# Moving cache gathers, patches and key turns in a four-layer residual kernel

## The chip, the core and the metric

The kernel runs on one core of a Trainium2 chip. The metric is device time in microseconds (us) of one launch. The kernel is written engine by engine: TensorE does matrix products and transposes, VectorE and ScalarE elementwise work and the copies out of PSUM, GpSimd some elementwise work and all gathers and scatters (indirect DMAs), and SyncE (SP) starts most of the plain DMAs; ScalarE starts some too.

## The reference

The input x has 64 sequences of 64 tokens of 512 numbers. Four layers are added to it one after the other, all in float32:

```python
x = x + einsum('bct,bcd->bdt', x, w0[cond])                 # one 64x64 mixer per sequence
x = x + x @ W_base.T + lora(x)                              # low-rank path picked per sequence
q, k, v = heads(x)                                          # 8 query heads, 4 key/value heads of 64
q, k = rope(rms(q)), rope(rms(k))
k_blocks = k_blocks.at[blk, :, off, :].set(k)               # new tokens written into a paged cache
v_blocks = v_blocks.at[blk, :, off, :].set(v)
x = x + softmax(mask(q @ k_all.T * SCALE)) @ v_all @ Wo.T   # window of 256 positions
x = x + x @ W3.T + low_rank3(x)
```

The cache is read through a table of 257 blocks of 16 positions per sequence. Sequences can share blocks, so a token written for one can be read by another. The mask leaves 256 positions, so for a sequence at most 21 blocks matter.

## The kernel before

The whole order of the work is written out by hand, and each engine runs its instructions in that order. An instruction that waits holds back everything behind it on its engine.

**First phase.** 39 rounds (line 882, n from 0 to 38) over tiles of 128 tokens, of which there are 32 (NTILE). Rounds 0 to 31 do the mixers and the first low-rank layer in groups of four, then keys and values (`product_kv`, line 815). The new rows of tile n - 1 are normalised and turned in the next round (`new_rows`, line 823) and scattered into two DRAM tables, pv and pk (`put_rows`, line 831), which hold a copy of every cache block that is written in this call. Those scatters are on GpSimd. Queries are done eleven rounds later: `product_q` (258), `norm_q` (266), whose last multiply (line 248) is on GpSimd for most tiles, and `turn_q` (276), which transposes them and writes them to DRAM (qd). Rounds 28 to 31 do no queries; rounds 32 to 38 do only queries.

**Cache reading.** For groups of four sequences, `k_load` (148) gathers old key blocks into kt, 84 rows of 8 KB per call, two calls per group. `k_copy` (154) reorders them into k2, a quarter at a time; the quarter with o4 = 3, and all of the first two groups, on ScalarE, others on VectorE. `k_patch` (161) gathers from pk over the rows of k2 that were written in this call. `k_turn` (169) transposes a quarter of one head pair into the one PSUM bank psK, and copies it into kT_mem, on ScalarE if o4 is even and on VectorE if it is odd. For one sequence, `v_load` (186) issues four gathers of values into vs_mem, which has two slots; `v_copy` (195) copies them on ScalarE into vt_mem, which has four slots; `v_patch` (199) gathers from pv over them; `v_share` (204) has SP issue three small DMAs within vt_mem.

**Second phase.** 128 steps (line 1117): a step is a sequence b and one of two pairs of key heads (gp), eight steps make a group q of four sequences, and i is the step within the group. In each step TensorE computes the scores of the next step (`scores`, 975), turns the shares of this one (`turn_p`, 1019), turns keys of the next group (`turn1`, then `turn2` further down, by the table in line 1114), does a part of the last layers of the group before (line 1144, `last_parts`), in the first two groups also the remaining queries, and at last multiplies shares by values (`values`, 1035). ScalarE and VectorE go along: `maxima` (990), `exponentials` (1004), `shares` (1011), `keep_p` (1028, the copy pT), `window` (967, the mask), `keep_o` (1045).

Of the kernel before, what the change touches and what calls it, by code (L numbers as in the profile page):

```python
# [21 lines left out]
NTILE = NT // P  # L22
# [28 lines left out]
def kernel(  # L51
# [89 lines left out]
    def bank(pool, name):  # L141
        return pool.tile([P, 512], F32, name=name, tag="b")
# [5 lines left out]
    def k_load(q, h):  # L148

        if q < B // 4:  # L150
            gather(kt[:NP, 2 * h : 2 * h + 2].rearrange("p g o d -> p (g o d)"), k_halves,
                   ik_old[:, h, q : q + 1])

    def k_copy(q, o4):

        if q < B // 4:
            (S.copy if o4 == 3 or q < 2 else V.tensor_copy)(
                k2[:NP].rearrange("p (oq o) g d -> p oq o g d", o=4)[:, :, o4],
                kt[:NP].rearrange("p g (oq o) d -> p oq o g d", o=4)[:, :, o4])

    def k_patch(q):

        if q < B // 4:
            gather(k2[:NP].rearrange("p o g d -> p (o g d)"), pk, ik_new[:, q : q + 1], NWR - 1)

    def kT(q, gp):
        return kT_mem[q % 2][:, gp].rearrange("p (b o c i) -> p b o c i", b=4, o=3, c=4)

    def k_turn(q, gp, o4, pool=psK):

        if q >= B // 4:
            return
        ps = bank(pool, f"psk{q}_{gp}_{o4}")[:, : 4 * NP].rearrange("p (o r) -> p o r", o=4)
        for oq in range(4):
            PE.transpose(ps[:, oq, :],  # L175
                         k2[:NP, 4 * oq + o4, 2 * gp : 2 * gp + 2].rearrange("p g d -> p (g d)"),
                         ident[:NP, :NP])
        if o4 < 3:
            dst = kT(q, gp)[:, :, o4, :3]
        else:  # L180
            dst = kT(q, gp)[:, :, :, 3]
        copy = V.tensor_copy if o4 % 2 else S.copy
        copy(dst[:, :, :, :NR], ps[:, :3].rearrange("p c (b j) -> p b c j", b=4))
        copy(dst[:, :, :, NR:], ps[:, 3].rearrange("p (b c j) -> p b c j", b=4, c=3))  # L184

    def v_load(b):
        if b < B:
            for g in range(NG):
                gather(vs_mem[:NV, b % 2, g].rearrange("p o d -> p (o d)"), v_rows,
                       iv_old[:, b, g : g + 1])  # L190
# [4 lines left out]
    def v_copy(b):  # L195
        if b < B:
            S.copy(vt(b)[:NV], vs_mem[:NV, b % 2].rearrange("p g o d -> p o g d"))  # L197

    def v_patch(b):
        if b < B:  # L200
            gather(vt_mem[:NV, b % 4], pv.rearrange("w (q r) -> (w q) r", q=4),
                   iv_new[:, b : b + 1], NWR * 4 - 1)

    def v_share(b):

        if b < B:
            for c in range(3):
                DMA.dma_start(out=vt(b)[96:NVK, c], in_=vt(b)[32 * c : 32 * c + 28, 3])
# [5 lines left out]
    def queries(n):  # L214

        return n - LQ if n < NTILE - 4 else -1 if n < NTILE else n - 4 - LQ
# [49 lines left out]
    def norm_q(n):  # L266

        if not 0 <= n < NTILE:
            return lambda: None
        rest = turned(n, psq.pop(n), NH, qsc, "q", qp1, qp2)  # L270

        def second():
            qheads[n] = rest()
        return second
# [19 lines left out]
    with ExitStack() as one:  # L294
# [587 lines left out]
        for n in range(NLAST):  # L882
            if n % 4 == 0:
                parts = first_parts(n // 4 + 1)
            w_load0(n + 12)
            x2_load(queries(n + 2))
            if 1 <= n <= NTILE:
                new_rows(n - 1)
            if n != NTILE:
                norm_q(queries(n - 1))()  # L890
            lag = 4 if n < 20 else 3 if n < 22 else 2 if n < 24 else 1
            while done["p"] <= min(n - lag, NTILE - 1):
                put_rows(done["p"])
                done["p"] += 1
            if n == NTILE:
                k_patch(0)
                v_patch(0)
                v_patch(1)
                norm_q(queries(n - 1))()
            product_q(queries(n), psP)  # L900
            if n % 4:
                x_load0(n + 8)
            if n in (14, 16, 18, 20):
                gather_indices((n - 14) // 2)
            if n < NTILE:
                parts[n % 4]()
            if n % 4 == 0:
                x_load0(n + 8)
            if n == 1:
                written_rows()  # L910
                places()
            if n in (1, 2):
                for o4 in (0, 1):
                    fill_copy(2 * (n - 1) + o4)
            if n == 2:
                fill_store(pv)
            if n >= 2:
                winners(n + 1 + max(0, (n - 6) // 4))
            if 2 <= n < 8:
                zero_rows((pk, pv)[n % 2], n // 2 - 1)  # L920
            if n in (13, 15, 17, 19):
                index_lists((n - 13) // 2)
            if n % 4 == 3:
                mixers(n // 4 + 2)
            if 5 <= n < 10:
                late_inputs(n - 5)
            if 14 <= n < 18:
                positions(n - 14)
            if n == 19:
                adapters(ad3_i, sc3b, 8, mask3)  # L930
                middles()
            if n == 21:
                residual3()
                G.memset(sm_mem, 0.0)
            turn_q(queries(n - 5 if n == NTILE else n - 2 if n != NTILE - 3 else -1), psO)
            if n < NTILE:
                product_kv(n)
            if n in (NTILE - 13, NTILE - 12):
                k_load(0, n - (NTILE - 13))
            if n in (NTILE - 11, NTILE - 9):  # L940
                v_load((n - (NTILE - 11)) // 2)
            if n in (NTILE - 7, NTILE - 5):
                v_copy((n - (NTILE - 7)) // 2)
            if NTILE - 8 <= n < NTILE - 4:
                k_copy(0, n - (NTILE - 8))
            if n in (NTILE - 3, NTILE - 2):
                k_load(1, n - (NTILE - 3))
            if n == NTILE - 4:
                v_load(2)


    def pool2(name, bufs):
# [5 lines left out]
    def q_load(q):  # L958
        if q < B // 4:
            qts[q] = ap2.tile([P, 2, 4, 2, T], F32, name=f"qs{q}", tag="qs")  # L960
            DMA.dma_start(out=qts[q], in_=qd[:, q])
# [73 lines left out]
    def values(s):  # L1035

        q, b, gp = steps[s]
        po = bank(psO, f"po{s}")[:, :P]
        for o in range(3):
            for g in range(2):  # L1040
                PE.matmul(po[g * HD : (g + 1) * HD, :], lhsT=vt(b)[:NVK, o, 2 * gp + g],  # L1041
                          rhs=pTs[s][g][:, o, :], start=(o == 0), stop=(o == 2))
        return po

    def keep_o(s, po):
        q, b, gp = steps[s]
        if s % 8 == 0:
            oTs[q] = ap2.tile([P, 2, 4, 2, T], F32, name=f"oT{q}", tag="oT")
        S.copy(oTs[q][:, gp, b % 4].rearrange("p h t -> p (h t)"), po)
# [59 lines left out]
    shares(0)  # L1109
    norm_q(nq - 1)()  # L1110
    window(1)
    for o4 in range(3):
        k_copy(1, o4)
    turns = {3: (None, (0, 0)), 4: ((1, 0), (0, 1)), 5: ((1, 1), (0, 2)), 6: ((1, 2), (0, 3)),
             7: ((1, 3), None)}
# [1 line left out]
    for s, (q, b, gp) in enumerate(steps):  # L1117
        i = s % 8
        turn1, turn2 = turns.get(i, (None, None))
        if i == 0 and q:  # L1120
            x_load(q)
        if i == 2:
            q_load(q + 1)
        if gp == 0:
            v_load(b + 3)
        else:
            v_share(b + 1)
            v_patch(b + 2)
        if i == 1:
            k_patch(q + 1)  # L1130
        if i in (2, 3):
            k_load(q + 2, i - 2)
        scores(s + 1)
        turn_p(s)
        if 0 < s < 16:
            turn_q(nq + s - 2, psO)
        if turn1:
            k_turn(q + 1, *turn1)
        maxima(s + 1)
        keep_p(s)  # L1140
        exponentials(s + 1)
        second = norm_q(nq + s if q < 2 else -1)
        if parts:
            parts.pop(0)()
        if q < 2:
            product_q(nq + s + 1, psM)
            x2_load(nq + s + 3)
        shares(s + 1)
        second()
        if gp:  # L1150
            window(b + 2)
        po = values(s)
        if turn2:
            k_turn(q + 1, *turn2)
        keep_o(s, po)
        if gp == 0:
            v_copy(b + 2)
        if i == 0:
            k_copy(q + 1, 3)
        elif i > 4:  # L1160
            k_copy(q + 2, i - 5)
        if i == 7:
            parts += last_parts(q)
    for part in parts:
# [52 lines left out]
```

## Time and profile before

| | |
|---|---|
| median of three runs | 1236.24 us (1232.07 to 1236.6) |
| the profiled execution | 1225.52 us, span 1223.7 us |
| TensorE busy | 1107.0 us, 90% of the span |
| VectorE, ScalarE, GpSimd busy | 753.0, 571.2, 613.9 us |
| value gathers (256, line 65) | 310.2 us of GpSimd, 1212 ns each |
| mean granted clock of TensorE | 0.976 |

The profiled execution is one run; its time is what its own lines add up to, and the median of the separate runs is 0.9% above it. Times within the profile are counted from the start of the span. In the slices each digit is the busy share of 30.6 us in tenths. A line of the timeline gives start, duration, engine, line of the kernel, operation, what is written and read, the number of instructions merged, and in brackets how long the engine sat idle before it and what ended that. The ends of TensorE's products are modelled, so its busy time is an upper bound. Gathers and scatters all carry line 65 or 71, since a helper issues them; they are told apart by their tiles: vs_mem for v_load, kt for k_load, k from pk for k_patch, vt_mem from pv for v_patch, pv and pk from va and k for the scatters.

### The profile page before, as it was taken

The page shows a single profiled execution, that of the slowest core. Times are in us where ns is not written, and L with a number is a line of the kernel's source. Part 1 is how long each engine was busy: PE and PEld are TensorE (multiplying, and loading weights), DVE is VectorE, ACT ScalarE, POOL GpSimd, SP SyncE. Part 2 cuts the span into 40 slices and gives each one's busy share as a digit, 9 for nine tenths or more (in the row PEclk, how much of TensorE's full clock was granted, in tenths as well). Part 3 has the DMA queues.
Part 4 walks back from the last instruction along what each step waited for, and adds up shares of the span by engine and source line. Part 5 has one row for each costly group of instructions (what it writes and reads, how often), then busy time and mean ns, then how long its engine had stood idle before and what let it go on. Part 6 is the DMA issues. An engine that isn't in the chain of part 4 may idle for free.

```text
span 1223.7 us, 17686 instructions
## 1 busy us (share of the span) xinstructions
PE 1107.0 (90%) x5622; PEld 639.8 (52%) x5622; DVE 753.0 (62%) x2313; ACT 571.2 (47%) x1472; POOL 613.9 (50%) x601
## 2 busy tenths in 40 slices
PE   4998899999999968879989989999999899999998
PEld 4434444444444434446656656555655565665665
DVE  3775346766666755875665655665665665666561
ACT  1332222232233324555655655655665565666651
POOL 3243323332543351887566666656656656656620
PEclk9999899999899988998999999999999999999999
DMA  8375713234331363546546556556555745756420
GB/s 270 123 258 209 241 41 113 74 102 131 111 114 51 108 171 111 157 117 147 129 113 161 130 126 143 147 126 142 147 127 140 167 121 121 161 139 150 99 64 35
DMA packets 129820, 163.20 MB, mean 133 GB/s; under 512 B 58079, under 2 KB 96891, under 8 KB 125545
## 3 DMA queue, kind: packets, MB, share of 16 engines
q0 software_dynamic: 63872, 85.04, 28.5%
q1 hardware_dynamic: 46416, 53.89, 14.5%
q10 hardware_dynamic: 19440, 23.15, 5.6%
q8 instruction: 45, 0.74, 0.3%
q14 instruction: 47, 0.39, 0.1%
HBM read 139.66 MB, written 50.33 MB: 155 GB/s over the span
## 4 chain that ended last, share of the span: by engine, by line
PE 66%; DVE 8%; issue 7%; DMA 6%; POOL 6%; ACT 3%; ACTq 0%; POOLq 0%; DVEq 0%; SPq 0%
PE pso L1059 9%; PE pp L1025 8%; PE po L1041 7%; PE psc L983 7%; PE ps L787 5%; PE psy L1084 5%; PE q L263 5%; PE kv L820 5%; PE psk L175 4%; PE psy L1078 4%; PE psxa L1067 2%; PE psy L1086 2%; DMA pv<-vt_mem,zidx 2%; POOL vs_mem L65 2%; PE ps L789 2%
## 5 line engine op out<-in xcount | busy, mean ns | idle before, releaser
L65 POOL DMA_INDIRECT vs_mem<-in_vblk_dram,iv_old x256 | 310.2, 1212 | 77.4 <-issue 70.5
L1009 ACT ACTIVATE sm_mem<-sm_mem,mn 128x336 f32<-128x336 f32 x256 | 145.6, 574 | 32.5 <-DVE mn L999 26.9
L65 POOL DMA_INDIRECT vt_mem<-pv,iv_new x64 | 80.0, 1250 | 160.2 <-ACT vt_mem L197 84.0
L999 DVE CUSTOM_DVE_ANT_0 sm_mem<-psc,pen 128x336 f32<-128x336 f32 x256 | 119.6, 501 | 43.6 <-PE pp L1025 22.8
L1041 PEld LDWEIGHTS po<-pT,vt_mem 124*64 124x64 f32 x1536 | 84.9, 137 | 87.0 <-ACT sm_mem L1009 49.2
L1041 PE MATMUL po<-pT,vt_mem 124*64 124x128 f32 x1536 | 118.4, 282 | 12.5 <-ACT pT L1032 7.3
L1059 PE MATMUL pso<-oT,woT_sb 128*128 128x256 f32 x512 | 123.2, 385 | 0.0
L263 PE MATMUL q<-wq_sb,x2q 128*128 128x512 f32 x256 | 120.8, 617 | 1.9 <-DMA x2q<-x2d 1.9
L1025 PE MATMUL pp<-ident,sm_mem 128*124 128x128 f32 x768 | 115.5, 283 | 6.8 <-issue 2.9
L1025 PEld LDWEIGHTS pp<-ident,sm_mem 128*124 128x124 f32 x768 | 81.3, 139 | 70.7 <-issue 58.6
L983 PE MATMUL psc<-kT_mem,qs 64*128 64x336 f32 x512 | 108.2, 498 | 10.7 <-DVE kT_mem L184 9.9
L787 PE MATMUL ps<-kT_mem,kT_mem 128*128 128x512 f32 x256 | 116.9, 600 | 0.6 <-PE ps_fill L493 0.6
L820 PE MATMUL kv<-wkv_sb,xr 128*128 128x512 f32 x256 | 115.4, 595 | 0.4 <-ACT va L828 0.4
L1017 DVE TENSOR_SCALAR sm_mem<-sm_mem,rsum 128x336 f32<-128x336 f32 x256 | 107.2, 419 | 9.1
L248 POOL TENSOR_TENSOR q<-q,rsq 128x512 f32<-128x512 f32 x30 | 31.5, 1050 | 139.7 <-DVE rsq L246 109.0
L1059 PEld LDWEIGHTS pso<-oT,woT_sb 128*128 128x128 f32 x512 | 92.5, 192 | 12.6 <-ACT pen L973 2.1
L175 PE MATMUL psk<-ident,k 84*128 84x84 f32 x512 | 63.8, 251 | 22.9 <-ACT kT_mem L184 9.1
L263 PEld LDWEIGHTS q<-wq_sb,x2q 128*128 128x128 f32 x256 | 50.0, 200 | 61.4 <-issue 61.2
L787 PEld LDWEIGHTS ps<-kT_mem,kT_mem 128*128 128x128 f32 x256 | 49.0, 193 | 61.5 <-issue 60.3
L1032 DVE COPY pT<-pp 124x384 f32<-124x384 f32 x128 | 70.8, 553 | 16.4 <-PE pp L1025 6.9
L1032 ACT COPY pT<-pp 124x384 f32<-124x384 f32 x128 | 61.6, 482 | 35.5 <-PE pp L1025 25.0
L820 PEld LDWEIGHTS kv<-wkv_sb,xr 128*128 128x128 f32 x256 | 46.9, 190 | 57.0 <-issue 55.5
(223 smaller groups left out, 1748.5 us busy)
## 6 DMA issues: line engine op xcount, KB each, us to landing
xt<-in_x_dram SPq DMA_DIRECT2D x32, 256.0 KB
x2d<-xr SPq DMA_DIRECT2D x8, 1024.0 KB
x2q<-x2d SPq DMA_DIRECT2D x32, 256.0 KB
qd<-qt ACTq DMA_DIRECT2D x64, 128.0 KB
qs<-qd SPq DMA_DIRECT2D x16, 512.0 KB
xq<-x2d SPq DMA_DIRECT2D x16, 512.0 KB
out_dram<-ys ACTq DMA_DIRECT2D x32, 256.0 KB
vt_mem<-vt_mem SPq DMA_DIRECT2D x192, 28.0 KB
```

The lines of the kernel that those rows point to most:

```text
L65: G.indirect_dma_start(out=dst, out_offset=None, in_=src, in_offset=bass.IndirectOffsetOnAxis(ap=idx, axis=0), **more,)
L175: PE.transpose(ps[:, oq, :], k2[:NP, 4 * oq + o4, 2 * gp : 2 * gp + 2].rearrange("p g d -> p (g d)"), ident[:NP, :NP])
L263: PE.matmul(psq[n], lhsT=xt[:, c, :], rhs=wq_sb[:, c, :], start=(c == 0), stop=(c == KC - 1))
L787: PE.matmul(ps, lhsT=wb_sb[:, c, oc * P : (oc + 1) * P], rhs=x1_mem[:, c, :], start=(c == 0), stop=False)
L820: PE.matmul(pskv[n], lhsT=xrs[s][:, c, i * P : (i + 1) * P], rhs=wkv_sb[:, c, :], start=(c == 0), stop=(c == KC - 1))
L983: PE.matmul(pscs[s][g], lhsT=qts[q][gs, gp, b % 4].rearrange("p h t -> p (h t)"), rhs=kT(q, gp)[gs, b % 4].rearrange("p o c i -> p (o c i) ...
L999: V.tensor_tensor_reduce(rows4(sm)[:, :, :, :28], rows4(pscs[s][g]), rows4(pens[b]), SCALE, 3.0e38, ALU.add, ALU.min, mn)
L1009: S.activation(w, w, AF.Exp, bias=mn, scale=-1.0, accum_out=rsum)
L1025: PE.transpose(pp[:NVK, o, :], sms[s][g][0][:, o * P : o * P + NVK], ident)
L1032: (V.tensor_copy if g else S.copy)(pT, pps[s][g][:NVK])
L1041: PE.matmul(po[g * HD : (g + 1) * HD, :], lhsT=vt(b)[:NVK, o, 2 * gp + g], rhs=pTs[s][g][:, o, :], start=(o == 0), stop=(o == 2))
L1059: PE.matmul(o, lhsT=woT_sb[:, c, ec * P : (ec + 1) * P], rhs=oT[:, c // 2, :, c % 2, :], start=(c == 0), stop=(c == 3))
```

## The change

Four moves, with the work itself unchanged:

- In the first phase, k_load(0) goes from rounds 19 and 20 to 16 and 17, k_copy(0) from rounds 24 to 27 to 19 to 22, k_load(1) from 29 and 30 to 23 and 24, v_load(0) and (1) from rounds 21 and 23 to 20 and 21, v_load(2) from 28 to 25; v_load(3) comes in at 26 (it was in the first step of the second phase). v_copy(0) and (1) go from 25 and 27 to 23 and 24, and v_copy(2) comes in at 28. v_patch(2) joins the patches in round 32.
- In the steps, values run one sequence further ahead: v_load(b + 4), v_copy(b + 3), v_patch(b + 3). v_share(b + 1) goes from the odd to the even step.
- k_patch goes from the second of eight steps to the first, and the last of the four k_copy from the first step to the eighth of the group before; for group 1 all four copies stand ahead of the steps.
- turn2 is put before the values in TensorE's order.

```diff
@@ -896,6 +896,7 @@
                 v_patch(1)
+                v_patch(2)
@@ -935,18 +936,16 @@
-            if n in (NTILE - 13, NTILE - 12):
-                k_load(0, n - (NTILE - 13))
-            if n in (NTILE - 11, NTILE - 9):
-                v_load((n - (NTILE - 11)) // 2)
-            if n in (NTILE - 7, NTILE - 5):
-                v_copy((n - (NTILE - 7)) // 2)
-            if NTILE - 8 <= n < NTILE - 4:
-                k_copy(0, n - (NTILE - 8))
-            if n in (NTILE - 3, NTILE - 2):
-                k_load(1, n - (NTILE - 3))
-            if n == NTILE - 4:
-                v_load(2)
+            if n in (NTILE - 16, NTILE - 15):
+                k_load(0, n - (NTILE - 16))
+            if n in (NTILE - 12, NTILE - 11, NTILE - 7, NTILE - 6):
+                v_load(n - (NTILE - 12) if n < NTILE - 10 else n - (NTILE - 9))
+            if n in (NTILE - 9, NTILE - 8, NTILE - 4):
+                v_copy(min(n - (NTILE - 9), 2))
+            if NTILE - 13 <= n < NTILE - 9:
+                k_copy(0, n - (NTILE - 13))
+            if n in (NTILE - 9, NTILE - 8):
+                k_load(1, n - (NTILE - 9))
@@ -1109,7 +1108,7 @@
-    for o4 in range(3):
+    for o4 in range(4):
         k_copy(1, o4)
@@ -1121,13 +1120,13 @@
+        if i == 0:
+            k_patch(q + 1)
         if gp == 0:
-            v_load(b + 3)
+            v_share(b + 1)
+            v_load(b + 4)
         else:
-            v_share(b + 1)
-            v_patch(b + 2)
-        if i == 1:
-            k_patch(q + 1)
+            v_patch(b + 3)
@@ -1149,16 +1148,16 @@
-        po = values(s)
         if turn2:
             k_turn(q + 1, *turn2)
+        po = values(s)
         keep_o(s, po)
         if gp == 0:
-            v_copy(b + 2)
-        if i == 0:
-            k_copy(q + 1, 3)
-        elif i > 4:
+            v_copy(b + 3)
+        if i > 4:
             k_copy(q + 2, i - 5)
+        if i == 7:
+            k_copy(q + 2, 3)
```

## The prediction

> **What bounds the kernel now.** I read the page's slices first, then TensorE's waits, then the timelines of the places where it waits.
>
> ```profile
> PE   4998899999999968879989989999999899999998
> PEclk9999899999899988998999999999999999999999
> PE 66%; DVE 8%; issue 7%; DMA 6%; POOL 6%; ACT 3%; ACTq 0%; POOLq 0%; DVEq 0%; SPq 0%
> PE psc L983 <- DVE kT_mem L184: 9.9, 15, 0.9
> PE pst L283 <- POOL q L248: 9.7, 1, 9.7
> ```
>
> The chain that ended last is TensorE for two thirds. Its one deep notch is the fifteenth slice (428 to 459 us, where the mixer rounds end and the attention steps are about to begin); the longest single wait (last line) lies there: a turn of queries waits 9.7 us for GpSimd. The line above it is a wait of 0.66 us that comes back in nearly every group of eight steps. What the change can win is in these two and beside them.
>
> The notch, on TensorE and then on GpSimd (start, duration, line, instruction, idle before):
>
> ```profile
> 441.99 0.60 PE L283 MATMUL pst<-ident,q 128*128 128x128 f32 x4
> 444.46 3.67 PE L263 MATMUL q<-wq_sb,x2q 128*128 128x512 f32 x8 [1.87 <-DMA x2q<-x2d]
> 457.79 1.12 PE L283 MATMUL pst<-ident,q 128*128 128x128 f32 x4 [9.65 <-POOL q L248]
> 458.69 4.62 PE L263 MATMUL q<-wq_sb,x2q 128*128 128x512 f32 x8
> ```
> ```profile
> 308.64 1.04 POOL L71 DMA_INDIRECT pv<-va,sidx  x1 [0.18 <-issue]
> 311.80 0.97 POOL L71 DMA_INDIRECT pv<-va,sidx  x1 [0.83 <-DMA pv<-va,sidx]
> ...
> 433.01 1.15 POOL L71 DMA_INDIRECT pv<-va,sidx  x1 [0.30 <-DMA pk<-k,sidx]
> ...
> 435.80 0.99 POOL L65 DMA_INDIRECT kt<-in_kblk_dram,ik_old  x1 [0.31 <-issue]
> 440.63 1.00 POOL L71 DMA_INDIRECT pv<-va,sidx  x1 [3.85 <-DMA pk<-k,sidx]
> ...
> 447.15 0.97 POOL L71 DMA_INDIRECT pv<-va,sidx  x1 [4.22 <-DMA pv<-va,sidx]
> ...
> 452.48 1.03 POOL L65 DMA_INDIRECT k<-pk,ik_new  x1 [3.08 <-DMA pk<-k,sidx]
> ...
> 456.68 2.05 POOL L248 TENSOR_TENSOR q<-q,rsq 128x512 f32<-128x512 f32 x2
> ```
>
> A scatter into pv waits until the one before it has landed. In round 20 two follow each other by 3.16 us. At the end of the rounds they take 7.6 and 6.5 us, because two key gathers, issued at 431.74 and 435.80 (k_load(1), rounds 29 and 30), share the DMA engines with them; before those, v_load(2) held GpSimd from 422.91 to 428.81. So the last scatter comes at 448.43, the patches at 452.48, and only behind them in GpSimd's order the multiply that TensorE needs:
>
> ```profile
> 439.00:442.00 3.00, 3.00 (x9) 1.28 (x8) 2.93 (x6) 1.00 (x3) 1.06 (x2) 1.00 1.07 252
> 451.00:454.00 3.00, 0.00 (x0) 0.00 (x0) 0.00 (x0) 0.00 (x0) 1.21 (x2) 0.50 0.01 3
> ```
>
> (Columns: TensorE, weight loads, VectorE, ScalarE, GpSimd busy; granted clock; DMA share; GB/s.) First DMA is full; then everything idles and the clock is 0.50.
>
> **Part 1, the gathers move to rounds 16 to 26.** Out of rounds 28 to 30 go v_load(2)'s four gathers and k_load(1)'s two. GpSimd then does only the scatters there. Tile 27's pv scatter stays at 420.25; tiles 28 to 31 follow every 3.2 us (the spacing of round 20; their rows are ready at 422.2, 424.9, 427.6, 430.3): the last pv at 433.1, the last pk at 434.4. From there 4.05 us to k_patch as now (448.43 to 452.48): 438.5. Then 1.34 us for it and three v_patch, one more than now (1.59, 1.59, 1.27 by the starts at 453.82, 455.41 and 456.68): the multiply at 444.3, done at 445.4. TensorE, with its 1.87 us wait for x2q gone (that load took from 434.88 to 444.46 under the key gathers; the load issued at 431.00 was in time), reaches the turn at 446.3: the wait of 9.65 vanishes whole. The clock comes on top: after the idling the turn took 1.12 for 0.60 and the next product 4.62 for 3.60, 1.54 us together. The Trainium skill, "TensorE: Matmul & The Clock Gate", Part 1, says that about 3.4 us of idling halve the clock and that about 3.4 us of work restore it; by that rule the loss is 1.7 us. I take the row. Sum 9.65 + 1.87 + 1.54 = 13.1 us. After that, products, turns and the load of qs follow each other as now.
>
> What pays for it: v_copy(2) now falls in round 28, ahead of the va copy for which the product at 420.41 waits: ScalarE's copy of 1.04 us, +1.0 (bounds 0 and 1.0). In rounds 16 to 26 GpSimd takes 6 us of value gathers in rounds 20, 21, 25 and 26; multiply, up to two pairs of scatters and gathers add to 13 us in round 20, which lasts 17 (multiplies at 307.42 and 324.34), and in round 26 end at 403.6, before the next multiply at 404.90. The same skill, "DMA: Bandwidth & Descriptors", section "Issuing engines are not separate DMA queues", speaks against the move: all queues run on the same 16 engines, so the gathers go on disturbing, only others. The row decides: the DMA share is 0.25 to 0.39 from 150 to 400 us, and x loads run eight rounds ahead. By the rule taken as in rounds 29 and 30 (the 1.87 us of x2q for two key gathers, and four of them move) it would be up to 3.7 us; I take 0.
>
> **Part 2, values one sequence ahead.** The loop's first even step still issues four gathers (v_load(4) for v_load(3)), so GpSimd, busy without a gap from 489.76 to 533 us, isn't relieved there; the four saved are at the end, where nobody waits. Load to copy stays two steps, copy to patch one. The slot written is that of b - 1, whose product ended a step before. v_share gets a step more after its patch and a step more before its product. On SP it stands earlier, ahead of x2_load; SP waits 327.7 us in 52 waits for patches to land from 560 to 1180, but neither qs nor x2q holds TensorE there. 0 us; without that cover a late share would cost its lateness once per sequence.
>
> **Part 3, k_patch in the first of eight steps, its last copy in the eighth.** In step 0 GpSimd, free at 489.56, must now wait for four copies of k2 on ScalarE instead of starting on values: three run from 487.42 to 490.34, a fourth to about 491.3. The values start at 492.7 instead of 489.76; k_patch's 1.33 us are gone from step 1: +1.6 us on GpSimd's full queue, which sets the end there. In the later groups the copy of 1.04 us leaves the first step, where no TensorE wait follows it, for the eighth, where ScalarE is late:
>
> ```profile
> 733.64 0.24 ACT L1049 COPY oT<-po 128x128 f32<-128x128 f32 x1
> 733.78 0.48 ACT L1032 COPY pT<-pp 124x384 f32<-124x384 f32 x1
> ...
> 734.99 0.97 PE L1041 MATMUL po<-pT,vt_mem 124*64 124x128 f32 x12
> ```
>
> pT would end at 735.3 instead of 734.26; the product waits 0.4 us. 13 groups: +5.2 us (bounds 0, and 1.04 each: 13.5).
>
> **Part 4, second key turn ahead of the values.** One group's end:
>
> ```profile
> 814.15 0.51 PE L175 MATMUL psk<-ident,k 84*128 84x84 f32 x4
> 814.69 0.42 DVE L183 COPY kT_mem<-psk 128x252 f32<-128x252 f32 x1 [0.38 <-PE psk L175]
> 815.32 0.84 PE L983 MATMUL psc<-kT_mem,qs 64*128 64x336 f32 x4 [0.66 <-DVE kT_mem L184]
> ```
>
> The turn moves up by the values' 0.8 us, but VectorE comes free only 0.38 before the copy: 0.38 of the 0.66 is won, in 12 of 14 groups (in two VectorE has no gap): -4.6. In the fourth step TensorE waits 0.6 to 1.2 us for pT in 9 groups and 0.3 to 1.8 in the fifth for the copy of that turn in 12; the turn (0.44 us) fills the first wait, and its copy can come earlier where ScalarE's window work lets it. Bounds per group 0 and 1.1; I take 0.5, nearer the 0.44 that surely fits: 13 times, -6.5. The wait of 0.45 in the seventh step stays: ScalarE's window precedes that copy.
>
> **Sum:** -13.1 + 1.0 + 1.6 + 5.2 - 4.6 - 6.5 = -16.4. The profiled execution took 1225.52 us, its span 1223.7; it would take 1209. The median of the runs is 1236.24, 0.9% higher; the same difference from it gives **1220 us**.
>
> **Rivals.** (B) The notch closes but the groups lose (the copy costs 0.8 each, the fourth step gives 0): -13.1 + 1.0 + 1.6 + 13 x 0.8 - 4.6 = -4.7; with the fourth step's gain between 0 and half of mine, 1228 to 1232. For: ScalarE's chain of window and copy sets several of these waits. Against: the 9.65 alone. (C) The scatters don't get faster, since 6 to 7 us is their own time for 1 KB rows: then pv goes out at 423.5 and three times 7 us later, 444.5 for 447.15 now: -2.6 + 1.6 for v_patch(2) + 1.0 + 1.6 - 5.9 in the groups = -4.3, 1232. For: 5.8 us still after 440.63. Against: 3.16 in round 20, and that the key gathers moved just then. (D) **Slower:** k_patch holds GpSimd until ScalarE's last copy of the eighth step (734.8), so the next four gathers are issued from 736.2 to 741.9 instead of 728.3 to 734.2, and the copy that needs them runs at 746.74 in ScalarE's order ahead of pT. A gather landed 1.0 us after its issue ended (571.43), another 2.2; a v_patch took 5.0 (728.00 to 733.05). Past 4.8 us every further us costs 13; from 6.1 us the sum is a loss: at 7.5 us, -16.4 + 35 = 1255. (E) The change does what it says but phase one pays with late x tiles: within C.
>
> **How the numbers follow.** No change can be told within 0.5%, 6.2 us. A, the sum, 0.64: 1220, own range 1211 to 1228. B 0.14, C with E 0.10, D 0.12. Faster: A and half of B, 0.71; same: the other half and C, 0.17; slower: D, 0.12. The range 1209 to 1236 leaves out D and the low tail of A; its upper end lies past B and C by the 4 us that the three runs differ among themselves.
>
> **What would show it.** Right: no wait of TensorE over 3 us from 430 to 460, granted clock 1.00 there, pv scatters 3.2 us apart, the first key turn about 12 us earlier; psc waits of 0.3; a new po wait of 0.4 in each first step; GpSimd waiting for k2's copy before k_patch. Wrong: scatters still 6 us apart (C), value copies of ScalarE waiting for gathers in the third step (D), or x2q and xt waits before 400 us.

## The result and the profile after

The kernel after takes 1301.16 us (median of four runs, 1291.66 to 1321.78), the kernel before 1236.42 beside it: ratio 1.049 (95% interval 1.039 to 1.059), **slower** by 5%, where 1220 was predicted. The experiments then fell on five chips, and these are of two kinds: on some the kernel before takes 1236 to 1244 us (the first kind; this comparison was made on one), on others 1199 to 1202 (the second kind). Each chip served for one set of runs only, so whether the difference belongs to the chip or to the hour isn't known; "kind" is a name for it. On the second kind the kernel after is 1.5% shorter than the kernel before (0.981 to 0.989). Both have to be explained. One execution each of e5 and e7 below is much faster than its three fellows (1280.70 us against 1303.63 to 1309.08, and 1260.64 against 1280.55 to 1284.29), so differences with these two are given by the medians and then by that fastest execution.

The page of the kernel after, its slices, its chain, and from TensorE's waits those that answer to the ones shown of before:

```profile
PE   4889799999999978788988977978979879789998
PEclk9999999998999989899999988989889889898999
PE 57%; DVE 12%; ACT 10%; issue 8%; DMA 5%; another core or an unknown queue 2%; POOL 1%; ACTq 1%; POOLq 0%; DVEq 0%; SPq 0%
```
```profile
PE po L1040 <- issue: 24.2, 30, 2.7
PE po L1040 <- ACT pT L1031: 19.2, 23, 3.6
...
PE pp L1024 <- issue: 12.8, 15, 3.1
...
PE psc L982 <- DVE kT_mem L184: 5.1, 15, 0.3
...
PE q L263 <- DMA x2q<-x2d: 2.6, 1, 2.6
```

The wait of 9.7 us for a turn of queries is gone, and the wait of the eighth step is down from 9.9 us to 5.1 in all. But the second half of the span, where before nearly every slice was a 9 at full clock, is now full of 7 and 8 with a clock below full: from 560 to 1190 us the granted clock is 0.50 in eleven stretches of 88.5 us together, in the kernel before in none. The profiled execution took 1305.27 us, its span is 1303.5 us, 79.8 longer than before; TensorE's busy time rose from 1107.0 to 1137.0 (+30.0, the same products at a lower clock: mean granted clock 0.954 for 0.976) and its idle time from 116.7 to 166.5 (+49.8).

**The notch** went much as predicted, on TensorE and on GpSimd:

```profile
445.43 0.60 PE L283 MATMUL pst<-ident,q 128*128 128x128 f32 x4
448.59 5.37 PE L263 MATMUL q<-wq_sb,x2q 128*128 128x512 f32 x8 [2.56 <-DMA x2q<-x2d]
...
458.11 1.04 PE L175 MATMUL psk<-ident,k 84*128 84x84 f32 x12
```
```profile
425.13 0.97 POOL L71 DMA_INDIRECT pv<-va,sidx  x1 [0.49 <-ACT va L828]
...
428.31 1.10 POOL L71 DMA_INDIRECT pv<-va,sidx  x1 [0.53 <-ACT sqk L226]
...
431.59 1.06 POOL L71 DMA_INDIRECT pv<-va,sidx  x1 [0.65 <-ACT qt L286]
...
435.86 1.17 POOL L65 DMA_INDIRECT k<-pk,ik_new  x1 [1.76 <-DMA pk<-k,sidx]
...
442.81 1.03 POOL L248 TENSOR_TENSOR q<-q,rsq 128x512 f32<-128x512 f32 x1 [0.98 <-DVE rsq L246]
```

The scatters are 3.2 us apart, k_patch comes at 435.86 for 452.48, the multiply at 442.81 for 456.68, and the turn waits for nothing. One wait stayed: a product still waits 2.56 us for x2q, and took 5.37 us for 3.60. The first key turn comes 9.3 us earlier than before (458.11 above); in the kernel before it was

```profile
467.45 1.04 PE L175 MATMUL psk<-ident,k 84*128 84x84 f32 x12
```

**The groups** of eight steps lost it again, several times over: from one k_patch to the next they last 46 to 55 us for 42 to 45. The start of one of them, GpSimd first, then TensorE, then ScalarE and VectorE:

```profile
885.78 1.25 POOL L65 DMA_INDIRECT vt_mem<-pv,iv_new  x1 [4.29 <-ACT pT L1031]
892.60 1.03 POOL L65 DMA_INDIRECT k<-pk,ik_new  x1 [5.58 <-PE pso L1058]
893.93 1.20 POOL L65 DMA_INDIRECT vs_mem<-in_vblk_dram,iv_old  x1 [0.30 <-issue]
...
898.42 1.34 POOL L65 DMA_INDIRECT vs_mem<-in_vblk_dram,iv_old  x1 [0.30 <-issue]
```
```profile
883.83 0.84 PE L982 MATMUL psc<-kT_mem,qs 64*128 64x336 f32 x4 [0.34 <-DVE kT_mem L184]
...
892.72 0.88 PE L1040 MATMUL po<-pT,vt_mem 124*64 124x128 f32 x12 [0.19 <-ACT pT L1031]
...
902.86 0.95 PE L1040 MATMUL po<-pT,vt_mem 124*64 124x128 f32 x12 [1.25 <-issue]
...
909.20 0.43 PE L1040 MATMUL po<-pT,vt_mem 124*64 124x128 f32 x2 [1.27 <-issue]
```
```profile
891.25 1.04 ACT L157 COPY k<-kt 84x1024 f32<-84x1024 f32 x1
...
906.80 0.27 ACT L1048 COPY oT<-po 128x128 f32<-128x128 f32 x1 [2.87 <-PE pp L1024]
907.03 1.05 ACT L197 COPY vt_mem<-vs_mem 92x1024 f32<-92x1024 f32 x1
```
```profile
906.84 0.51 DVE L998 CUSTOM_DVE_ANT_0 sm_mem<-psc,pen 128x336 f32<-128x336 f32 x1 [1.60 <-PE pp L1024]
...
918.23 0.51 DVE L998 CUSTOM_DVE_ANT_0 sm_mem<-psc,pen 128x336 f32<-128x336 f32 x1 [3.94 <-remote]
```
```profile
890.00:900.00 10.00, 9.51 (x68) 6.77 (x69) 7.42 (x23) 6.77 (x17) 5.95 (x5) 1.00 0.77 210
900.00:910.00 10.00, 6.80 (x44) 4.73 (x42) 4.44 (x15) 4.79 (x13) 8.10 (x7) 1.00 0.38 92
910.00:920.00 10.00, 9.13 (x33) 6.52 (x34) 3.57 (x13) 3.50 (x13) 5.82 (x6) 0.50 0.88 176
```

Three things are to be seen. **The hold:** GpSimd reaches k_patch at 887 and sits 5.58 us until ScalarE's copy (891.25) is done; the line names a product, but the copy writes the rows of k2 that k_patch writes over, and it ended just before (892.29). Over the run this is 80.7 us in 13 waits, and the value gathers stand behind it. **Late results:** ScalarE starts oT at 906.80, 3 us after the last recorded end of its product (the po group that began at 902.86 and took 0.95), and VectorE begins the next maxima at the same moment. Both engines were free, and both waited for TensorE. **Half clock:** in 900 to 910 TensorE is busy for 6.80 of 10 us, with no gap over 1.27, and then runs at 0.50 for ten. Eleven such stretches make 88.5 us; at half speed they cost at most 44 of the 79.8 us (an estimate: half of their time, as if TensorE were busy in all of it).

In the kernel before such late results are there too on this chip, about once a group, 13 times of 14 in the third step. One of them (the product, ScalarE's oT, and the next product, all of before):

```profile
743.30 0.88 PE L1041 MATMUL po<-pT,vt_mem 124*64 124x128 f32 x12
746.53 0.27 ACT L1049 COPY oT<-po 128x128 f32<-128x128 f32 x1 [3.00 <-PE pp L1025]
748.58 0.43 PE L1041 MATMUL po<-pT,vt_mem 124*64 124x128 f32 x2 [0.70 <-issue]
```

Adding up, for each step, by how much oT starts later than both the recorded end of its product and the end of ScalarE's earlier work, the kernel before has 35.8 us with 14 cases over 1 us, the kernel after 59.3 us with 18.

### The profile page after: what moved, and what is told of

Same layout as the page of the kernel before. It is cut to its first block, busy times and chain, and to the rows that moved or that the text cites. A ratio compares the mean times of both kernels' runs of the same rounds, so it can differ in the third digit from the quotient of the medians.

```text
span 1303.5 us, 17740 instructions
## 1 busy us (share of the span) xinstructions
PE 1137.0 (87%) x5622; PEld 665.6 (51%) x5622; DVE 761.4 (58%) x2313; ACT 573.0 (44%) x1472; POOL 614.8 (47%) x601
## 4 chain that ended last, share of the span: by engine, by line
PE 57%; DVE 12%; ACT 10%; issue 8%; DMA 5%; another core or an unknown queue 2%; POOL 1%; ACTq 1%; POOLq 0%; DVEq 0%; SPq 0%
PE pso L1058 6%; PE po L1040 6%; PE pp L1024 6%; PE q L263 6%; PE psc L982 5%; PE ps L787 5%; PE kv L820 4%; PE psy L1083 4%; PE psxa L1066 3%; PE psk L175 3%; PE psy L1077 3%; PE psy L1085 2%; DVE sm_mem L1016 2%; DMA pv<-vt_mem,zidx 2%
## 5 line engine op out<-in xcount | busy, mean ns | idle before, releaser
L1040 PE MATMUL po<-pT,vt_mem 124*64 124x128 f32 x1536 | 127.1, 287 | 47.6 <-issue 24.2
L1024 PE MATMUL pp<-ident,sm_mem 128*124 128x128 f32 x768 | 122.5, 292 | 34.7 <-issue 12.8
L1024 PEld LDWEIGHTS pp<-ident,sm_mem 128*124 128x124 f32 x768 | 84.9, 144 | 104.7 <-issue 81.4
L1040 PEld LDWEIGHTS po<-pT,vt_mem 124*64 124x64 f32 x1536 | 89.7, 139 | 94.1 <-issue 40.9
L982 PE MATMUL psc<-kT_mem,qs 64*128 64x336 f32 x512 | 111.9, 513 | 5.9 <-DVE kT_mem L184 5.1
L1016 DVE TENSOR_SCALAR sm_mem<-sm_mem,rsum 128x336 f32<-128x336 f32 x256 | 110.5, 432 | 9.1
L1058 PEld LDWEIGHTS pso<-oT,woT_sb 128*128 128x128 f32 x512 | 92.9, 193 | 12.7 <-ACT oT L1048 2.7
L1048 ACT COPY oT<-po 128x128 f32<-128x128 f32 x128 | 33.6, 263 | 133.3 <-PE po L1040 72.5
L972 ACT ACTIVATE pen<-pen,edge 128x336 f32<-128x336 f32 x64 | 36.8, 576 | 104.9 <-DVE pen L971 65.0
L175 PEld LDWEIGHTS psk<-ident,k 84*128 84x128 f32 x512 | 53.4, 148 | 53.0 <-issue 25.3
```

Source lines behind the costliest of these rows:

```text
L982: PE.matmul(pscs[s][g], lhsT=qts[q][gs, gp, b % 4].rearrange("p h t -> p (h t)"), rhs=kT(q, gp)[gs, b % 4].rearrange("p o c i -> p (o c i) ...
L1016: V.tensor_scalar(w, w, rsum, None, ALU.mult)
L1024: PE.transpose(pp[:NVK, o, :], sms[s][g][0][:, o * P : o * P + NVK], ident)
L1058: PE.matmul(o, lhsT=woT_sb[:, c, ec * P : (ec + 1) * P], rhs=oT[:, c // 2, :, c % 2, :], start=(c == 0), stop=(c == 3))
```

## The experiments

Four or more runs of each, beside the kernel before on the same chip. A time can be set against another only within its kind of chip. Where no interval stands, the ratio is that of the medians, with that of the fastest execution behind it.

| run | what differs | kind | us | before | ratio (95%) |
|---|---|---|---|---|---|
| e1 | first-phase moves alone | 2 | 1187.74 | 1198.66 | 0.991 (0.988-0.993) |
| e2 | e1 and values ahead | 2 | 1187.94 | 1198.66 | 0.992 (0.988-0.995) |
| e3 | e1 and k_patch's part | 2 | 1212.11 | 1198.66 | 1.012 (1.007-1.017) |
| e4 | e1 and turn2 | 2 | 1197.42 | 1198.66 | 0.998 (0.995-1.002) |
| e5 | the whole change | 1 | 1305.33 | 1244.03 | 1.049; 1.029 |
| e6 | whole, without k_patch's part | 1 | 1212.82 | 1244.03 | 0.976 (0.969-0.984) |
| e7 | whole, without values ahead | 1 | 1281.33 | 1244.03 | 1.030; 1.013 |
| e8 | whole, k_patch behind the gathers | 1 | 1217.08 | 1244.03 | 0.979 (0.972-0.986) |
| e9 | whole, fourth copy early | 2 | 1179.48 | 1201.79 | 0.981 (0.976-0.985) |
| e10 | e8 and e9 together | 2 | 1179.36 | 1201.79 | 0.981 (0.976-0.986) |
| e11 | whole, k_patch back, copy not | 2 | 1185.19 | 1201.79 | 0.987 (0.982-0.991) |
| e12 | e6 again | 2 | 1190.58 | 1201.79 | 0.989 (0.985-0.992) |
| e13 | the whole change again | 2 | 1182.60 | 1200.19 | 0.985 (0.981-0.989) |
| e14 | whole, gathers behind k_patch left out | 2 | 1177.60 | 1200.19 | 0.980 (0.976-0.984) |
| e16 | e9 again | 2 | 1182.92 | 1200.19 | 0.986 (0.982-0.990) |
| e17 | whole, hold taken away | 2 | 1194.99 | 1200.19 | 0.995 (0.993-0.997) |
| e18 | e8 with the gathers split | 1 | 1195.77 | 1238.11 | 0.962 (0.956-0.968) |
| e19 | e8 again | 1 | 1206.60 | 1238.11 | 0.973 (0.969-0.976) |

**The four parts (e1 to e4).** e1 has the moves of rounds 16 to 26 without v_load(3), v_copy(2) and v_patch(2), which belong to the values; e2 adds these and the values' lines of the steps. The edits of e3 and of e4, both on top of e1 (the text of e4 below says that it is the kernel before with turn2 alone, but the kernel that ran has the moves of the first phase too, so its measure is e1):

```diff
-    for o4 in range(3):
+    for o4 in range(4):
         k_copy(1, o4)
...
+        if i == 0:
+            k_patch(q + 1)
...
-        if i == 1:
-            k_patch(q + 1)
...
-        if i == 0:
-            k_copy(q + 1, 3)
-        elif i > 4:
+        if i > 4:
             k_copy(q + 2, i - 5)
+        if i == 7:
+            k_copy(q + 2, 3)
```
```diff
-        po = values(s)
         if turn2:
             k_turn(q + 1, *turn2)
+        po = values(s)
```

> The first-phase moves alone; the steps are those of the kernel before (the fourth value load and the third value copy and patch stay in the steps). The changed kernel reached its first key turn 9.3 us earlier than the kernel before, and lost about 6 us in each group of eight steps. Theories T1 (k_patch and its copy moved), T2 (values one sequence ahead), T3 (turn2 ahead of the values): the loss is none of this part's, so this runs 9 us faster than before, about 1227 us, ratio 0.992, groups 44.4 us apart. Theory T4 (the first-phase moves leave the steps with gathers in another place): 1280 or more, groups 49 us apart.

> The first-phase moves and values one sequence ahead (with v_share in the even step); k_patch, its copy and turn2 as before. T2 (the shares stand a step earlier in SP's queue, so q_load and the gathers of a step fall on the DMA engines at the same time): 1280 to 1300 us, ratio 1.04 or more, gathers' and shares' stretches with TensorE idle. T1 or T3: about 1228, ratio 0.993.

> The first-phase moves, k_patch in the first of eight steps and its last copy in the eighth; values and turn2 as before. T1 (k_patch waits on GpSimd some 6 us for ScalarE's copy, and the value and key gathers behind it then run back to back for 25 us): 1280 to 1300 us, ratio 1.04 or more, groups 49 us apart. T2 or T3: 1228 to 1234 (my 5.2 us for the copy at most), ratio 0.993 to 0.998.

> The kernel before with turn2 ahead of the values, nothing else. T3 (the turn delays the values and with them oT, and its copies queue ahead of pT): 1260 or more, ratio above 1.02. T1 or T2: 4.6 to 11 us faster by my working (the eighth step's wait 0.66 to 0.3 us, the fourth and fifth steps 0.5 us per group), 1225 to 1232, ratio 0.991 to 0.996.

Measured: 10.9 us won by the first-phase moves, nothing more or less by the values, 24.4 us lost by k_patch's part (1212.11 against 1187.74), and 9.7 us lost by turn2 (1197.42 against 1187.74; of its twelve executions two, at 1183.40 and 1185.82, lose nothing, and the profiled one is the second of these). T2 and T4 fall; T1 and T3 hold in sign, T1 with some third of the loss of the first comparison and T3 with a seventh.

In e3 the path of the loss is plain (the profiled execution, 1222.58 us, is the longest of the five). SP's queue, GpSimd's last gather of the first step, ScalarE's copy of what was gathered, and TensorE:

```profile
724.04 0.54 SPq L959 DMA_DIRECT2D qs<-qd  x1
```
```profile
729.22 1.19 POOL L65 DMA_INDIRECT vs_mem<-in_vblk_dram,iv_old  x1 [0.30 <-issue]
```
```profile
736.93 1.04 ACT L197 COPY vt_mem<-vs_mem 92x1024 f32<-92x1024 f32 x1 [3.83 <-DMA vs_mem<-in_vblk_dram,iv_old]
```
```profile
738.40 0.88 PE L1039 MATMUL po<-pT,vt_mem 124*64 124x128 f32 x12 [2.32 <-ACT pT L1030]
```

The gathers end 6.5 us after the last one's issue ended (730.41), the copy waits 3.83 us for them, pT stands behind the copy on ScalarE, and the product waits for pT. Over the run this is

```profile
PE po L1039 <- ACT pT L1030: 24.5, 24, 3.2
```

for 3.5 us in e1. This is the mechanism of rival D.

**The whole change and single parts taken back, on the first kind (e5 to e8).** e6 undoes e3's diff, e7 the values' lines; e8 keeps k_patch in the first step and only changes its place in it:

```diff
-        if i == 0:
-            k_patch(q + 1)
         if gp == 0:
             v_share(b + 1)
             v_load(b + 4)
         else:
             v_patch(b + 3)
+        if i == 0:
+            k_patch(q + 1)
```

> The changed kernel whole, once more, beside the parts of it. On the chip of the first four runs the kernel before took 1198.66 us (1236.42 in the first comparison), the k_patch part lost 22 to 24 us against the first-phase moves alone and the other parts nothing. Theory U (the parts add up): 0.9905 + 0.021 and nothing for the others: ratio 1.01, about 1212 us if the kernel before takes 1199. Theory W (the parts multiply: values ahead and turn2 make k_patch's hold worse): ratio 1.03 to 1.05.

> The changed kernel with k_patch and the fourth key copy back in their places of before; the three other parts stay. If the whole loss is k_patch's: ratio 0.985 to 0.99 (first-phase moves 0.9905, turn2 0.998, values 1.00), no wait of ScalarE's value copies for their gathers. If values ahead or turn2 lose by themselves in company: above 1.00.

> The changed kernel with values, v_share and their loads as before; first-phase moves, k_patch and turn2 stay. Theory U: ratio 1.01, as the k_patch part without turn2 (1.012). Theory W with values as the partner: ratio 1.01 here and 1.03 or more for the whole change; with turn2 as the partner: 1.03 or more here too.

> The changed kernel with k_patch still in the first of eight steps and its last copy still in the eighth, but issued behind that step's four value gathers instead of ahead of them. If the loss comes from the gathers that GpSimd issues late because k_patch ahead of them waits for ScalarE's copy: value gathers go out 6 us earlier, ScalarE's value copies don't wait for them (34.9 us in 14 waits with k_patch ahead), and the loss is gone: ratio 0.985 to 0.99. If the loss comes from the copy in the eighth step (1.04 us of ScalarE, my 5.2 us) or from k_patch falling together with other transfers: above 1.00.

The whole change lost 61 us here by the medians, near the 65 of the first comparison, and 37 by the fastest execution. Without k_patch's part it wins 31 us, so that part costs 92 us (68 by the fastest); behind the gathers it costs 4 us, within the runs' scatter. So the order of k_patch and four gathers on GpSimd decides over some 88 us (64 by the fastest). One such place in e8, the first of the four gathers and then k_patch:

```profile
894.95 1.20 POOL L65 DMA_INDIRECT vs_mem<-in_vblk_dram,iv_old  x1 [0.30 <-issue]
...
900.97 1.01 POOL L65 DMA_INDIRECT k<-pk,ik_new  x1 [0.30 <-DMA vt_mem<-vt_mem]
```

The hold before k_patch fell from 5.8 us a group to 0.4, since the gathers ahead of it fill the time. TensorE's busy time fell back from 1138.6 to 1098.8 us (e6: 1095.8), and its time at half clock between 560 and 1190 us from 71.4 to 20.4 (e6: 3.4). Values taken back (e7) bring 24 of the 61 us (20 by the fastest), the hold staying at 5.8: they make it worse here, but aren't the cause. What e8 can't tell is whether the hold costs or the order alone: e17 below keeps the order and takes the hold away, but fell on the second kind.

**The hold shortened (e9, e10), the copy's price (e11, e12).** These fell on the second kind. e9 moves the fourth copy up within the eighth step:

```diff
         if turn1:
             k_turn(q + 1, *turn1)
+        if i == 7:
+            k_copy(q + 2, 3)
...
-        if i == 7:
-            k_copy(q + 2, 3)
```

e10 does this and e8's edit; e11 is the whole change with k_patch back in the second step; e12 is e6.

> The changed kernel with one copy moved within the eighth step: k_copy(q + 2, 3) stands behind that step's first key turn, ahead of the copy pT, instead of at the step's end. k_patch stays ahead of the value gathers. If what costs is the time for which k_patch holds GpSimd (5.8 us in 14 groups of the changed kernel), the copy ends some 4 us earlier, the hold falls to about 1 us and the loss goes with it: ratio 0.98 to 0.99. If what costs is that k_patch is issued ahead of the value gathers at all, or in the same step: ratio above 1.00, near that of the changed kernel (1.05 on the chip of the last four runs).

> Both mends: the copy early in the eighth step and k_patch behind the first step's value gathers. If the copy at the end of the eighth step still costs 0.4 us a group (5.2 us, a step of my prediction), this is 5 us better than k_patch behind the gathers alone (0.979 then): ratio 0.975; if it cost nothing there, the same as that: 0.979.

> The changed kernel with only k_patch back in the second of eight steps; its last copy stays at the end of the eighth. Prices the copy's place by itself: by my prediction 5.2 us more than the kernel with both back (ratio 0.976 on its chip), 0.980; with nothing lost there, 0.976; if the copy and not the hold made the loss, above 1.00.

> The changed kernel with k_patch and the copy both back, once more, as the measure for the three others on their chip: ratio 0.976 (0.969 to 0.984 before) if the chip is like the one of the last four runs, 0.985 to 0.99 if it is like the one of the first four.

e9's reading failed: the hold stayed at 5.3 us, because VectorE's copy of the third quarter, at the end of the same step, now ended last. It looked like a cure against e3, but e13 shows that the whole change is about as fast here (0.985, and e9's repeat 0.986). What stands is e11 against e12: the copy at the end of the eighth step costs nothing that can be measured (0.987 and 0.989), where 5.2 us were predicted.

**The whole change on the second kind (e13), the hold taken away (e17), e9 again (e16), the gathers left out (e14).** e17, on top of e9, and e14, in which one sequence in four works on values of an earlier one:

```diff
-        if i > 4:
+        if i in (5, 6):
             k_copy(q + 2, i - 5)
+        if i == 6:
+            k_copy(q + 2, 2)
```
```diff
         if gp == 0:
             v_share(b + 1)
-            v_load(b + 4)
+            if i or q == 0:
+                v_load(b + 4)
```

> The changed kernel whole, beside its mends on one chip. On the chip where the kernel before takes 1240: ratio 1.05 again. On the chip where it takes 1200 the whole change has not run yet: if the hold of GpSimd costs what it cost there with the first-phase moves (24 us against them), 0.989 + 0.02 = 1.01; if values ahead and turn2 make it worse, 1.03 or more; if turn2 makes up for it, 0.98 to 1.00.

> The changed kernel with k_patch still ahead of the value gathers, but nothing left for it to wait for: the third quarter's copy (VectorE) at the end of the seventh step, the fourth's (ScalarE) behind the eighth step's key turn. The hold of GpSimd falls from 5.8 us to about 1 us a group and the gathers behind it go out 5 us earlier. If the hold is the cause: ratio 0.975 to 0.98, no waits of the value copies for gathers. If it is k_patch's being in the same step as these gathers, or ahead of them: no better than the kernel with only the fourth copy early.

> The changed kernel with only the fourth copy early in the eighth step, once more. The hold stayed at 5.3 us in its first run, since VectorE's copy of the third quarter, at the end of the same step, then ended last; k_patch went out only some 0.6 to 1.2 us earlier, yet the value copies waited 16.3 us for gathers instead of 34.9, and the ratio was 0.9805. On the same kind of chip: 0.98 again. On the chip where the kernel before takes 1240: if each us of the hold past a bound counts, as in my rival D, a gain of some 15 to 25 us on the whole change, ratio 1.03; if the last us decides, below 1.00.

> The changed kernel without the four value gathers that stand behind k_patch in each group's first step (from the second group on), so that one sequence in four works on old values; k_patch, its hold and all else stay. If the loss comes through these gathers landing late for ScalarE's copy: it is gone, ratio 0.98 or less. If the loss comes from the hold itself in another way (v_patch and the other gathers queued behind it, or k_patch beside other transfers): it stays in good part, more than half of what the whole change loses on this chip against the mended kernels.

Here the whole change is 17.6 us faster than before. The hold is there in full (5.8 us), and costs next to nothing: leaving out the very gathers that it delays brings 5 us, no more than the scatter of the runs. Three of the four places shown of e3, in e13:

```profile
713.72 0.54 SPq L960 DMA_DIRECT2D qs<-qd  x1
```
```profile
721.51 1.19 POOL L65 DMA_INDIRECT vs_mem<-in_vblk_dram,iv_old  x1 [0.30 <-issue]
```
```profile
726.06 1.05 ACT L197 COPY vt_mem<-vs_mem 92x1024 f32<-92x1024 f32 x1 [0.67 <-DMA vs_mem<-in_vblk_dram,iv_old]
```

The gathers end 3.4 us after the last one's issue ended (722.70), not 6.5, and the copy waits 0.67 us for them (10.5 us in 12 waits, for 34.9 in 14 in e3). In e3 the load of qs (512 KB) is issued 0.65 us behind k_patch (723.39) and just ahead of these gathers (724.73 to 730.41); in e13 it went out 1.95 us ahead of k_patch (715.67), since with the values ahead the share before it comes sooner on SP. e3's own groups bear this out, with the same code in all: in seven of the 13 the load is issued behind k_patch (by 0.23 to 1.45 us), and the copy starts 5.9 to 7.4 us after the last gather's issue ended; in the other six it is issued ahead (by 0.24 to 0.90), and the copy starts after 3.1 to 5.4. In e13 it is ahead in all 13, by 1.4 to 2.0, and the copy starts after 2.8 to 5.0. No run moves that load alone.

e17's hold fell to 0.75 us, and the kernel got slower (0.995): now products wait for shares, which they never do in e13:

```profile
PE po L1040 <- DMA vt_mem<-vt_mem: 10.2, 11, 2.2
```

So on the second kind it isn't the hold that matters, and taking it away by crowding the copies costs more than it. e16 repeats e9: no better than the whole change.

**k_patch behind the gathers once more, and the gathers split (e19, e18), on the first kind.**

```diff
-            v_load(b + 4)
+            v_load(b + 4, (0, 1))
         else:
             v_patch(b + 3)
+            v_load(b + 4, (2, 3))
```

> The changed kernel with k_patch behind the first step's value gathers, once more. It was at 0.979 on the chip where the kernel before takes 1240 (the whole change 1.05 there) and has not run where the kernel before takes 1200 (the whole change 0.985 there). If the order of k_patch and these gathers matters only where TensorE's results come late in the third step: 0.98 to 0.985 on the 1200 chip; 0.979 again on the 1240 chip.

> The same, with each sequence's four value gathers split, two in the even and two in the odd step. On the 1240 chip TensorE's results came late (by 2 to 4 us, once or twice a group) near the end of a train of four or more value gathers on GpSimd. If the trains make them late: on that chip 15 to 30 us better than with the gathers together, late results gone. If not: no better, and the copies, which have one step less, wait for gathers. On the 1200 chip, which has no late results: no better, 0 to 10 us worse.

e19 repeats e8 (0.973 and 0.979). Splitting each sequence's four gathers over two steps brings 10.8 us more, less than expected, and the late results go: 12.7 us in all and no case over 1 us, for 27.2 us and 7 cases in e19 and 33.3 us and 13 in e8, the same kernel. But the split didn't make trains of two: the second pair of one step and the first pair of the next still stand back to back, and between 560 and 1160 us four value gathers follow each other in 41 of GpSimd's 51 unbroken runs. What got rarer are runs of 12 gathers, 17.5 us without a break: 4 for 12 in e19. It does so although ScalarE's copies now wait for their gathers:

```profile
ACT vt_mem L197 <- DMA vs_mem<-in_vblk_dram,iv_old: 24.4, 14, 3.4
```

e18, at 0.962, is the best of all on this kind: 42 us faster than the kernel before. Neither it nor e8's edit alone was run on the second kind; e10, which has e8's edit, was, at 0.981.

## Why the prediction was wrong

**Part 1 was right in the main.** The notch closed by the steps given: scatters 3.2 us apart, the wait of 9.65 gone. The multiply came 1.5 us earlier than worked out (442.81 for 444.3). v_copy(2) cost what was written: the product behind it waits 1.50 us, where 0.44 stood before. One term was not kept: a wait for x2q stayed, 2.56 us with 1.77 us of slow product, at a product whose load was in time before. So 9.3 us were won at the first key turn, where 13.1 less 1.0 were expected. e1 measures 10.9 us for the moves alone. Weighed there was what the Trainium skill says in "DMA: Bandwidth & Descriptors", section "Issuing engines are not separate DMA queues", that all queues run on the same 16 engines: I took 0 and the bound was 3.7. The runs lie nearer to the bound: the DMA share was still 0.87 at 446 to 449 us, and 4.3 us went there; e1 won 10.9 of 13.1. That the moved gathers made this load late isn't shown.

**Part 2**, values ahead at 0 us: right by itself (e2 against e1: 0.2 us). But it isn't by itself here: together with k_patch's part the values ahead make things worse on the first kind (e7 against e5: 24 us, 20 by the fastest), while on the second the qs load, 2.6 us earlier against k_patch in the groups shown, since the share's move on SP, seems to help.

**Part 3 is the step that failed.** It priced the two ends of the move, ScalarE's copy in the eighth step (+5.2) and step 0 (+1.6), and left out of the sum what lies between: GpSimd standing still before k_patch in every group, with the value gathers queued behind. Rival D named it and gave it 0.12. The trace has the hold (80.7 us in 13 waits), and e8 shows that k_patch's place among these gathers is worth 88 of the 92 us on this kind of chip (64 of 68 by the fastest execution). By what path is not shown. What the trace shows is that with the hold GpSimd issues in fewer and longer unbroken runs: nine of 17 gathers (some 24.8 us each) between 560 and 1160 us, where before most had 5 to 7. On the second kind runs of 22 do no harm (e13). The term that was priced is hardly there: the product in the first step waits 0.19 us, not 0.4 (892.72 above), and e11 against e12 finds no cost. Step 0 went as written (GpSimd waits 2.04 us for k2's copy; values from 482.32).

**Rival D** had the right place and the wrong path for this chip. It said that the copies wait for gathers past 4.8 us after their issue. In the kernel after, on the first kind, no copy waits for a gather: 907.03 above comes 7.3 us after the last gather's issue ended, but directly behind an oT that was itself late by TensorE's result. On the second kind D's path is what e3 shows, and what the whole change just escapes, with 3.4 us to land.

**Part 4** was right about the wait that it named and wrong in the sum: 11.1 us were to be won, and e4 against e1 loses 9.7. In the profiles the eighth step's wait falls from 10.8 us (e1) to 6.4 (e4): 4.4 us, for 4.6 predicted. But turn2, moved up, meets something not looked at: k_patch's gather from the second step has not landed. Two rows of TensorE's waits, of e1 and then of e4:

```profile
PE psk L175 <- DMA k<-pk,ik_new: 8.5, 7, 2.8
```
```profile
PE psk L175 <- DMA k<-pk,ik_new: 16.4, 11, 3.7
```

That is 7.9 us more, which eats the gain. It is not shown to be the loss: the profiled execution of e4 has this wait and is 1.9 us shorter than that of e1. With k_patch in the first step the wait is gone altogether (none in e13; 13.8 us in 11 waits in e12), a gain of Part 3 that the prediction didn't list either.

**The sum.** -16.4 us was predicted; on the second kind the whole change gives -17.6, and that is luck. The parts measured one by one there give -10.9 + 0.2 + 24.4 + 9.7 = +23.4, so that 41 us come from their company: k_patch's part and turn2 each lose with the first-phase moves alone and don't lose together with the values. A sum of parts priced one by one can't show this. On the first kind the change gives +61 to +65 (+37 by the fastest execution of e5), and nothing in the sum stands for what differs there: a TensorE whose results were already late once a group, in a trace that I had read. ScalarE's three microseconds of idling before oT at 746.53, and the two "issue" waits of the product just behind it (0.70 and 0.34 us), were in the trace of before and went unexplained. I had worked out what a late gather costs a waiting copy, not what the longer runs of gathers would meet there.

**What stays open.** Why the two kinds differ. On the first kind the late results go when the gathers are split, so where the gathers stand has a part in them; by what way, no run shows. Whether there the hold costs or only the order was not parted either. Nor can the late results alone be the loss: e6 has 49.5 us of them in 15 cases and is the fast one. In the whole change they come with a TensorE that idles in pieces and falls to the half clock, in e6 they don't; which of the two sets off the other was not parted.

## What to carry to other kernels

When a gather is moved up on an in-order engine, price what waits behind it while it waits, not only the instruction and its data: here, on one kind of chip, four gathers behind one held patch decided 64 to 88 us, and putting the patch behind them cured it. Explain an idle stretch in the trace of before, however small, before you put more transfers there. Measure the parts of a change in company as well as one by one: here they don't add up. And try a change of a few per cent on more than one chip: here its sign differs between them.

## What the runs showed of the hardware

- Two kinds of chips (or of hours): the kernel before takes 1236 to 1244 us on one and 1199 to 1202 on the other. In e6 and e12, the same kernel on either, the instructions take the same times by their medians and the first k_patch of the steps comes at 492.4 and 493.2 us; after the first group, the groups then take 42.5 to 44.7 and 39.6 to 44.6 us. Late results add up to 12.7 to 59.3 us in the kernels on the first kind and to 2.8 to 3.5 us on the second, with no single one over 0.3 us.
- On the first kind results of TensorE reach ScalarE up to 4.4 us after the recorded end (e19), at 906.80 of the kernel after together with VectorE. All 67 cases over 1 us in the kernel before, e6, e8, e19 and the kernel after come with five or more gathers issued back to back on GpSimd. With the gathers of each sequence split over two steps (e18) no case is over 1 us, though most runs of gathers are still five or more.
- Where the load of qs (512 KB) was issued behind k_patch, the four gathers behind it were late for their copy: it started 5.9 to 7.4 us after the last issue ended, and 3.1 to 5.4 us where the load went ahead (e3, 7 and 6 groups).
- The clock of the kernel after fell to 0.50 at 910.1 us after ten microseconds in which TensorE was idle for 3.2 us in pieces, none over 1.27 by the records, and stayed there for ten, though TensorE was busy for 9.13 of them by the records.
